# A graph layer and a mixture of experts in one program: three expert blocks move in among the node groups

## The chip, the cores and the metric

The program runs on one core of a Trainium2 chip. The metric is the device time of one execution, in microseconds (us); the kernel before takes 1253.61 us (median of three runs).

Engines: PE (TensorE, matmuls; its weight loads are shown as PEld), DVE (VectorE), ACT (ScalarE), POOL (GpSimd; it issues the indirect transfers) and SP (SyncE; it issues most of the plain transfers). Each engine takes its instructions strictly in the order in which the program lists them.

## The reference

What is computed, cut to what matters (6250 nodes, 100000 edges sorted by their target node `dst`):

```python
h = layernorm(x)                                  # 6250 x 256
s, cnt = segment_sum(edge, dst), segment_count(dst)   # edge: 100000 x 96
mx = where(cnt > 0, segment_max(edge, dst), 0)
z = concat([h, s, mx, s / max(cnt, 1), u[0]], 1)  # 256 + 3*96 + 64 = 608
x = x + (relu(z @ W1 + b1) @ W2 + b2 + h)         # hidden size 1024
q = layernorm(x)
v, idx = top_k(q @ gate_w + gate_b, 2)            # 16 experts
w = softmax(v)
f = [relu(q @ w1[e] + eb1[e]) @ w2[e] + eb2[e] for e in range(16)]  # 256 -> 512 -> 256
y = q + w[0] * f[idx[0]] + w[1] * f[idx[1]]
out = x + (layernorm(y) * gamma + beta)
```

## The kernel before, in words

**Node groups.** The 6250 nodes are 50 columns of P = 125. They are worked on in 13 groups of four columns (group 0 has two), and each group has 12 slots of a written schedule: slots 0 to 7 are `hidden` (L779 for 512 of the 544 inputs that differ from node to node, L796 for the last 32, the ReLU on ACT at L801; the 64 global inputs are folded into the bias once, `global_part`), slots 8 to 11 are `output` (L807), one column each. Around these stand the things that a group needs before it and does after it: the load of x (`take_x`, slot B - 17, with B the group's first slot), its layernorm (L717 scales a column into `xn` on ACT), two gathers per column on POOL (`take_edges` L737 into the tile `at`, `take_carry` L744 into `cg`), their join on DVE (`join_edges`, L750) and masking on ACT (`mask_edges`, L757), the five transposes (`turn`, L770) with ACT's copies into `inT` (L771); afterwards the residual on DVE (`residual`, L812), the second layernorm (`root_b` L821, `turn_b` L837), the gate's logits (`logits`, L845), the choice of two experts (`choose`, L852 to L860, with an exponential on ACT at L860), the place of each node among its experts' rows (`rank`, `rank_2`, `place`), and `send`, which scatters each node's row to its two experts' row buffers `xg_d` (POOL, L906).

**Edges.** DVE runs a stream of edge chunks beside this: running sums and maxima along runs of equal targets (L318 to L322, tiles `raw` and `rw`, in three buffers, each result stored to `rows_d`). At the end of each of seven regions a chain joins the runs: ACT's copies into `ct` (L394), transposes on PE (L406, L408), copies and a scan on DVE (L419, L423), transposes back (L432), DVE's correction (L438, L440) and a store of `carry_d` (L442), which later gathers read. Also spread among the groups is the search for the nodes' edges: `find_block` (ACT, L488), `take_blocks` (DVE, L492, and a POOL gather, L501), `find_edge` (ACT, L508), and `bounds`, `bounds_2` (PE, L526) and `index_nodes` (DVE, L642, reads PE's `pg` into `end`).

**The order** is written out by hand. Every piece is entered with a slot and, for some, a cost in DVE time; the entries are sorted by slot and listed in that order for all engines, and before each next slot the edge stream gets DVE time up to a credit of 4.6 us per slot:

```python
            at_slot(B + HC + i, output, g, i)
...
        tasks.sort(key=lambda t: t[:2])
...
            fn(*args)
            credit -= cost
```

**Experts.** All rows of an expert are worked on in blocks of SB = 256. `find_star` picks one favoured expert (the star) early; its rows are renumbered to stand first, and once groups 0 to 10 are counted (`count_full`, `take_full`) its first NA = 14 blocks can be run before the other experts' sizes are known. From the last output on, `run_block` takes one block after another, software-pipelined: `load_rows` (L1041: a register load on SP, then 263 KB from `xg_d`), `load_weights` (1026 KB, once for the star, for each block of another expert), `norm_block` (ACT), `turn_block` (L1074, copied at L1077), `first_layer` (L1192), `second_layer` (L1214), `own_place` (DVE, L1086 and L1087 for the star's weights `w`), `weigh` (DVE, L1115), `store_y` (SP, L1120), and then, for blocks of the others, the partner row of each row from `y_d`, the last layernorm and the scatter to `out`. A loop after the pipeline (`extra_block`) takes what blocks are left beyond the NS = 57 planned ones.

**Buffers.** PSUM has one bank for transposes (`pTp`) and five for accumulation (`acc`); `ld` holds `at` (two buffers), `xall` holds XB = 5 buffers of x, `wk` holds `xn` (one buffer) and `inT`.

## Time and profile before

| | |
|---|---|
| three runs | 1251.32, 1253.61, 1262.72 us; median 1253.61 |
| profiled execution | 1255.86 us; span on the core 1254.0 us |
| mean granted TensorE clock | 0.958 |
| busy: PE, PEld | 1103.0 us (88%), 784.4 us (63%) |
| busy: DVE, ACT, POOL | 976.0 us (78%), 603.8 us (48%), 565.8 us (45%) |
| HBM | 146.70 MB read, 121.75 MB written, 214 GB/s over the span |
| star's and others' first layer, L1192 | 912 matmuls, 206.8 us |
| second layer, L1214 | 912 matmuls, 208.8 us |
| groups' hidden layer, L779 | 832 matmuls, 367.2 us |
| groups' output, L807 | 800 matmuls, 190.2 us |
| first `hidden` of groups 3, 5, 6 | 247.6, 368.4, 428.4 us |
| last output ends | 800.9 us |

How to read it. Times of rows are from the start of the profiled span; the profiled execution took 1.9 us more than its span. The page's second part cuts the span into 40 slices of 31.35 us and gives the busy share of each engine as a digit in tenths. A row of the timeline is the start, the busy time, the engine, the line, the operation with out<-in, the shapes and the number of records; what stands in brackets is idle time ahead of it and what ended it. In the view of waits each row is a waiter and what it waits for, then the total in us, the count and the longest. A row of the chain is a start, a length and the work. "Releasers" are worked out from semaphore events. PE's matmuls are pipelined, so a busy PE is not always at its peak.

### The profile page before, as it was taken

To read this page: it belongs to the slowest core of one execution; us is meant where nothing else is said; L and a number is where in the kernel's file an instruction comes from. 1 tells how busy PE (TensorE), PEld (TensorE's weight loads), DVE (VectorE), ACT (ScalarE), POOL (GpSimd) and SP (SyncE) were. 2 spreads that over 40 slices of the span, in tenths; PEclk is the share of its full clock that TensorE was granted. 3 is DMA by queue.
4 is the path that set the end of the run, shared out by engine and by line. 5 is a ranking of instruction groups with operands and counts; after the bars stand their busy time and mean duration, and the time that the engine had idled before them with its cause. 6 is when DMAs were issued, how large, how long until landed. Compare 5 with 4: busy or idle time off the path is not lost.

```text
span 1254.0 us, 16849 instructions
## 1 busy us (share of the span) xinstructions
PE 1103.0 (88%) x4637; PEld 784.4 (63%) x4637; DVE 976.0 (78%) x2820; ACT 603.8 (48%) x1410; POOL 565.8 (45%) x721
## 2 busy tenths in 40 slices
PE   1594796997978888899999999999999999999983
PEld 1372363646454645466464665788888888888873
DVE  4689786996989888899989931355458888888985
ACT  3473252644255642434234252343367677766752
POOL 5121151673338673353733351303026666656664
PEclk9997899998989998999999999999999999999997
DMA  6959785787698898788999723113478889888972
GB/s 163 213 131 249 193 245 157 197 213 233 171 267 247 260 249 238 216 233 247 254 259 278 189 65 91 49 63 106 140 232 233 250 281 295 278 246 276 300 235 76
DMA packets 179318, 260.86 MB, mean 208 GB/s; under 512 B 35899, under 2 KB 145947, under 8 KB 173585
## 3 DMA queue, kind: packets, MB, share of 16 engines
q1 hardware_dynamic: 140097, 201.97, 56.3%
q0 software_dynamic: 39008, 57.35, 16.5%
q8 instruction: 37, 0.61, 0.2%
q14 instruction: 64, 0.52, 0.1%
q10 hardware_dynamic: 112, 0.41, 0.1%
HBM read 146.70 MB, written 121.75 MB: 214 GB/s over the span
## 4 chain that ended last, share of the span: by engine, by line
PE 40%; DVE 5%; DMA 5%; issue 1%; ACT 1%; POOL 0%; SPq 0%; another core or an unknown queue 0%; POOLq 0%; DVEq 0%
PE acc L1192 13%; PE acc L1214 13%; PE acc L779 6%; PE acc L807 4%; PE pT L1074 2%; DMA cg<-carry_d,next_i 2%; DMA xt<-in_x_dram 1%; DMA y_d<-yb 1%; PE pg L845 1%; PE acc L796 1%; DMA rows_d<-rw 0%; PE pT L770 0%; DMA g<-y_d,from_i 0%; DVE bsc L1142 0%; DVE yb L1115 0%
## 5 line engine op out<-in xcount | busy, mean ns | idle before, releaser
L779 PE MATMUL acc<-inT,w1x 128*128 128x500 f32 (+1 forms) x832 | 367.2, 589 | 4.8 <-DVE xt L812 4.8
L779 PEld LDWEIGHTS acc<-inT,w1x 128*128 128x128 f32 x832 | 158.7, 199 | 164.8 <-issue 150.9
L906 POOL DMA_INDIRECT xg_d<-xt,pos_i x100 | 135.1, 1351 | 249.1 <-issue 92.4
L1214 PE MATMUL acc<-wt,hb 128*128 128x256 f32 x912 | 208.8, 382 | 4.3 <-ACT hb L1200 4.1
L1192 PE MATMUL acc<-xT,wt 128*128 128x256 f32 x912 | 206.8, 380 | 1.6 <-DVE xT L1077 1.6
L807 PE MATMUL acc<-w2s,hT 128*125 128x256 f32 x800 | 190.2, 393 | 0.0
L1192 PEld LDWEIGHTS acc<-xT,wt 128*128 128x128 f32 x912 | 172.7, 190 | 25.1 <-DVE xT L1077 1.8
L1214 PEld LDWEIGHTS acc<-wt,hb 128*128 128x128 f32 x912 | 169.8, 191 | 26.8 <-ACT hb L1200 5.0
L807 PEld LDWEIGHTS acc<-w2s,hT 128*125 128x125 f32 x800 | 153.2, 196 | 24.8 <-issue 1.9
L1129 POOL DMA_INDIRECT g<-y_d,from_i x86 | 91.5, 1064 | 155.1 <-DMA y_d<-yb 134.3
L1200 ACT ACTIVATE hb<-acc,wt 128x256 f32<-128x256 f32 x200 | 84.0, 471 | 122.8 <-PE acc L1192 90.4
L501 POOL DMA_INDIRECT gb<-in_dst_dram,blk_i x50 | 75.7, 1514 | 98.8 <-ACT xt L725 41.7
L1165 POOL DMA_INDIRECT out_dram<-g,to_i x86 | 93.5, 1087 | 22.5 <-issue 18.3
L801 ACT ACTIVATE hT<-acc,c 128x500 f32<-128x500 f32 (+1 forms) x104 | 60.3, 662 | 71.5 <-PE acc L796 71.4
L1115 DVE SCALAR_TENSOR_TENSOR yb<-acc,w_b,xe 128x256 f32<-128x256 f32 x112 | 48.9, 478 | 47.5 <-PE acc L1214 38.3
L321 DVE TENSOR_TENSOR rw<-rw,raw 125x768 f32<-125x768 f32 x88 | 83.8, 952 | 0.2 <-issue 0.2
L322 DVE TENSOR_TENSOR rw<-rw,raw 125x768 f32<-125x768 f32 x88 | 83.6, 950 | 0.0
L318 DVE TENSOR_TENSOR rw<-rw,keep 125x768 f32<-125x768 f32 x81 | 76.8, 948 | 8.1 <-DMA rows_d<-rw 8.1
L744 POOL DMA_INDIRECT cg<-carry_d,next_i x44 | 64.0, 1455 | 33.8 <-issue 11.6
L737 POOL DMA_INDIRECT at<-rows_d,first_i x44 | 61.7, 1401 | 34.0 <-issue 20.5
L319 DVE TENSOR_TENSOR rw<-rw,bar 125x768 f32<-125x768 f32 x81 | 77.0, 950 | 0.0
L771 ACT COPY inT<-pT 128x500 f32<-128x500 f32 (+1 forms) x65 | 36.2, 556 | 83.0 <-PE pT L770 74.1
(324 smaller groups left out, 1591.4 us busy)
## 6 DMA issues: line engine op xcount, KB each, us to landing
wt<-in_wpack_dram SPq DMA_DIRECT2D x44, 1026.0 KB
rows_d<-rw SPq DMA_DIRECT2D x46, 960.0 KB
rows_d<-rw SPq DMA_DIRECT2D x46, 540.0 KB
raw<-in_edge_dram SPq DMA_DIRECT2D x46, 480.0 KB
xb<-xg_d SPq DMA_DIRECT2D x57, 263.0 KB
y_d<-yb SPq DMA_DIRECT2D x56, 256.0 KB
raw<-in_edge_dram SPq DMA_DIRECT2D x46, 270.0 KB
xt<-in_x_dram SPq DMA_DIRECT2D x12, 500.0 KB
```

What stands on the lines that cost most here:

```text
L318: nc.vector.tensor_tensor(su, prev[0], keep[c][:, :, s + j, None].to_broadcast(bcast), op=OP.mult)
L319: nc.vector.tensor_tensor(mx, prev[1], bar[c][:, :, s + j, None].to_broadcast(bcast), op=OP.min)
L321: nc.vector.tensor_tensor(su, su, x_j, op=OP.add)
L322: nc.vector.tensor_tensor(mx, mx, x_j, op=OP.max)
L779: nc.tensor.matmul(G[g]["pH"][m % 4][:, :n * P], w1x[:, k, m * 128:(m + 1) * 128], inT[:, k, :n * P], start=(k == 0), stop=False)
L807: nc.tensor.matmul(pO, G[g]["hT"][m][:, i * P:(i + 1) * P], w2s[:, m, :], start=(m == 0), stop=(m == HC - 1))
L906: d = nc.gpsimd.indirect_dma_start(out=xg_d[:, :], out_offset=IndirectOffsetOnAxis(ap=G[g]["pos"][:, i, k:k + 1], axis=0), in_=G[g]["xt"][ ...
L1129: d = nc.gpsimd.indirect_dma_start(out=g[:, h, :].bitcast(I32), out_offset=None, in_=y_d[:, :], in_offset=IndirectOffsetOnAxis(ap=BL[b]["f ...
L1165: d = nc.gpsimd.indirect_dma_start(out=out[:, :], out_offset=IndirectOffsetOnAxis(ap=BL[b]["to"][:, h:h + 1], axis=0), in_=BL[b]["g"][:, h ...
L1192: nc.tensor.matmul(pB[:, i, :], wt[:, k * FF + m * 128:k * FF + (m + 1) * 128], xT[:, k, :], start=(k == 0), stop=(k == DC - 1))
L1200: nc.scalar.activation(hb[:, m, :], pB[:, i, :], AF.Relu, bias=bias)
L1214: nc.tensor.matmul(to, hb[:, m, h * 128:(h + 1) * 128], wt[:, W2O + m * D:W2O + (m + 1) * D], start=(m == 0), stop=(m == FC - 1))
```

## The change

Three blocks of the star run among the node groups, one each in groups 3, 5 and 6 (`EARLY`), as entries of the schedule. In slot 3 of such a group `pick_early` counts the star's rows so far on PE and DVE and moves on by a block if there are enough; in slot 4 `load_early` loads that block's rows on SP; `norm_early` (ACT, and DVE for the weights), `turn_early`, `first_early` (two halves) and `second_early` (two halves of the rows) stand between slots 8.5 and 11.5, between the group's outputs; `store_early` issues the store of the block from ACT's queue. In `second_early` PE adds the row (a matmul with the identity) and the bias (a matmul of one contracted row) into the accumulator, where `weigh` does this on DVE for later blocks. These blocks use the transpose bank, the accumulation banks, and tiles of their own or of `gT`, `xn`.

The star now has NA = 17 blocks planned, 3 early and 14 after the groups; NS stays 57, so 40 others follow where 43 did. Its weights are loaded in slot 28 (`load_star`) into a tile that stays. `take_full` is done in two parts (the first 10 of the 14 blocks from the count of groups 0 to 10, the others from that of groups 0 to 11, after the last group's outputs are listed). To make room, x has four buffers where it had five, `at` one where it had two; the fill of the row buffers uses the early blocks' row tile. The weights of the global part (`w1u`) are loaded by SP into a buffer of `inT` later on, and the global part's matmuls and addition stand after the window sums.

```diff
-NA = 14
+KE = 3
+NA = KE + 14
+N1 = 10
+EARLY = (3, 5, 6)
 NS = 57
...
-XB = 5
+XB = 4
...
-    ld = mlp.enter_context(tc.tile_pool(name="ld", bufs=2))
+    ld = mlp.enter_context(tc.tile_pool(name="ld", bufs=1))
...
     def max_window(g, i):
         w = G[g]["win"][i]
+        if "at" not in G[g]:
+            G[g]["at"] = ld.tile([P, GS, 128 * (KC - DC + 1)], F32, name="at")
...
+    def load_star():
+        nc.vector.memset(done, float(SB))
+        e = nc.sync.value_load(star_i[0:1, 0:1], min_val=0, max_val=NE - 1)
+        nc.sync.dma_start(eba, eb2[ds(e, 1), :].to_broadcast([128, D]))
+        nc.sync.dma_start(wta, wpack[ds(e * 128, 128), :])
+
+    def pick_early(g):
+        pc = eps.tile([NR, NE], F32, name="ps")
+        nc.tensor.matmul(pc, ones[:P, :NR], M[:, NT - GRP[g - 2][0], :], start=True, stop=True)
+        nc.vector.tensor_scalar(more_f, pc[:, 0:1], done, float(SB), op0=OP.is_ge, op1=OP.mult)
+        nc.vector.tensor_add(done, done, more_f)
+        nc.vector.tensor_scalar(at_a, done[0:1], float(-2 * SB), 0.0, op0=OP.add, op1=OP.max)
+
+    def load_early():
+        EB["r"] = r = nc.sync.value_load(at_a[0:1, 0:1], min_val=0, max_val=(NA - 1) * SB)
+        nc.sync.dma_start(xba, xg_d[ds(r, SB), :].rearrange("(p h) d -> p h d", h=2))
+
+    def norm_early():
+        for h in range(2):
+            nc.scalar.activation(xba[:, h, 0:D], xba[:, h, 0:D], AF.Identity, scale=xba[:, h, D + 5:D + 6], bias=xba[:, h, D + 6:D + 7])
+        nc.vector.scalar_tensor_tensor(wea, xba[:, :, D + 2], float(N), xba[:, :, D + 1], op0=OP.is_ge, op1=OP.add)
+        nc.vector.tensor_tensor(wea, wea, xba[:, :, D], op=OP.min)
+
+    def turn_early():
+        pX = pTp.tile([128, DC, 2, 128], F32, name="pT")
+        for k in range(DC):
+            for h in range(2):
+                nc.tensor.transpose(pX[:, k, h, :], xba[:, h, k * 128:(k + 1) * 128], ident)
+        xT = gtp.tile([128, DC, GS * P], F32, name="gT", bufs=1).rearrange("p k n -> p (k n)")[:, 0:DC * SB]
+        EB["xT"] = xT.rearrange("p (k r) -> p k r", r=SB)
+        nc.scalar.copy(xT, pX.rearrange("p k h r -> p (k h r)"))
+
+    def first_early(half):
+        if half == 0:
+            EB["hb"] = wk.tile([128, GS, D], F32, name="xn", bufs=1)
+        pB = acc().rearrange("p (i r) -> p i r", i=2)
+        for i in range(2):
+            m = 2 * half + i
+            for k in range(DC):
+                nc.tensor.matmul(pB[:, i, :], wta[:, k * FF + m * 128:k * FF + (m + 1) * 128], EB["xT"][:, k, :],
+                                 start=(k == 0), stop=(k == DC - 1))
+            nc.scalar.activation(EB["hb"][:, m, :], pB[:, i, :], AF.Relu, bias=wta[:, B1O + m:B1O + m + 1])
+
+    def second_early(h):
+        if h == 0:
+            EB["pY"] = acc().rearrange("p (h d) -> p h d", h=2)
+        to = EB["pY"][:, h, :]
+        nc.tensor.matmul(to, ident, xba[:, h, 0:D], start=True, stop=False)
+        nc.tensor.matmul(to, ones[0:1, :], eba[0:1, :], start=False, stop=False)
+        for m in range(FC):
+            nc.tensor.matmul(to, EB["hb"][:, m, h * 128:(h + 1) * 128], wta[:, W2O + m * D:W2O + (m + 1) * D],
+                             start=False, stop=(m == FC - 1))
+        nc.scalar.activation(xba[:, h, 0:D], to, AF.Copy, scale=wea[:, h:h + 1])
+
+    def store_early():
+        EB["ra"] = nc.scalar.value_load(at_a[0:1, 0:1], min_val=0, max_val=(NA - 1) * SB)
+        d = nc.scalar.dma_start(y_d[ds(EB["ra"], SB), :].rearrange("(p h) d -> p h d", h=2), xba[:, :, 0:D].bitcast(I32))
...
-    def take_full():
-
-        full, nbi = MB["full"], MB["nbi"]
-        nc.vector.memset(full, 0.0)
-        nc.vector.tensor_copy(nbi, MB["pc"])
...
+    def take_full(a, z):
+
+        nbi, tf, last, top = MB["nbi"][:, 0:1], MB["tab_f"][:, a:z], MB["last"], MB["q"]
+        nc.vector.tensor_copy(nbi, MB["pc"][:, 0:1])
         nc.vector.tensor_scalar(nbi, nbi, 8, None, op0=OP.arith_shift_right)
...
+        nc.vector.tensor_scalar(top, nbi, 1.0, -1.0, op0=OP.mult, op1=OP.add)
...
+        nc.vector.tensor_scalar(tf, row_i[0:1, 0:z - a], last[0:1], top[0:1], op0=OP.add, op1=OP.min)
+        nc.vector.tensor_scalar(MB["tab_a"][:, a:z], tf, 0.0, float(SB), op0=OP.max, op1=OP.mult)
...
-                at_slot(max(0, B - 17), take_x, g)
+                at_slot(max(9, B - 17), take_x, g)
...
+        if g in EARLY:
+            for q, fn, *a in ((3, pick_early, g), (4, load_early), (8.5, norm_early), (9, turn_early), (9.5, first_early, 0),
+                              (10, first_early, 1), (11, second_early, 0), (11.5, second_early, 1), (12, store_early)):
+                at_slot(B + q, fn, *a)
...
+    at_slot(T, count_full, NG - 2)
+    at_slot(T + 1, take_full, N1, NA - KE)
+    at_slot(T, first_blocks, KE, NS)
+    for b in range(KE, NA):
+        at_slot(T + 1.6 * (b - KE), run_block, b, NS)
...
+        fill = xba[:, 0, :]
...
+    at_slot(SLOTS * EARLY[0] - 8, load_star)
...
-        nc.gpsimd.dma_start(w1u, w1[D + 3 * EF:D + 3 * EF + GF])
...
-        global_part()
+        w1u = wk.tile([128, KC + 1, GS * P], F32, name="inT").rearrange("p k n -> p (k n)")[:GF, 0:HID]
+        nc.sync.dma_start(w1u, w1[D + 3 * EF:D + 3 * EF + GF])
...
+        ps_u = global_part(w1u)
...
+        nc.vector.tensor_add(c1, ps_u, b1c)
```

## The prediction

> **What bounds the kernel now.** I read the page first: busy shares, then the 40 slices.
>
> ```profile
> PE 1103.0 (88%) x4637; PEld 784.4 (63%) x4637; DVE 976.0 (78%) x2820; ACT 603.8 (48%) x1410; POOL 565.8 (45%) x721
> DVE  4689786996989888899989931355458888888985
> PEclk9997899998989998999999999999999999999997
> ```
>
> The program has two stages: slices 6 to 22 are the node groups (DVE 8 to 9 tenths), after 800 us come the expert blocks. The page's average hides that they have different limits, so I cut the span into windows: group 5, group 9, and 227 us of late expert blocks (columns: length, busy time of PE, PEld, DVE, ACT, POOL, clock, DMA share, GB/s).
>
> ```profile
> 368.40:428.40 60.00, 51.05 (x194) 30.35 (x193) 50.87 (x128) 33.69 (x87) 41.77 (x39) 0.97 0.91 253
> 596.60:646.10 49.50, 48.46 (x194) 29.42 (x193) 48.44 (x106) 19.73 (x41) 23.66 (x26) 1.00 0.93 262
> 913.00:1140.00 227.00, 226.00 (x1108) 198.72 (x1108) 189.35 (x621) 156.23 (x361) 133.44 (x233) 1.00 0.85 263
> ```
>
> In the expert stage PE stands still for 1.0 of 227 us. The chain that ended last gives one block there:
>
> ```profile
> 1113.46 3.45 PE acc L1192 x16
> 1116.91 0.44 PE pT L1074 x4
> 1117.35 3.46 PE acc L1214 x16
> 1120.80 3.45 PE acc L1192 x16
> ```
>
> 3.45 + 0.44 + 3.46 = 7.35 us, and nothing but PE in it. In groups 3 to 7 neither engine is full, so I read who waits for whom between 368 and 486 us:
>
> ```profile
> DVE at L750 <- DMA cg<-carry_d,next_i: 11.0, 7, 3.6
> ACT dv L860 <- DVE I L857: 10.9, 1, 10.9
> PE pT L770 <- ACT inT L771: 8.9, 3, 4.0
> ```
>
> PE waits for ACT's copies, ACT waits (in its order) for DVE, DVE only for gathers: DVE leads and PE runs behind it by permission. PE idles 5.4 + 9.0 + 5.4 us in groups 3, 5 and 6. An extra PE task is free there as long as no DVE instruction that reads a PE result gets there first. That slack decides this case.
>
> **What goes.** Three expert blocks leave the PE-bound stage: 54 run after the groups instead of 57, still 14 of the favoured expert first, so 40 others instead of 43: 3 x 7.35 = -22.05 us. The loop after the pipeline stays empty by the reference's own routing: the favoured expert has 4831 rows (18 whole blocks, 17 taken), the rest need 40. Three 1026 KB weight loads go too; they lie under PE.
>
> **What comes, on PE.** Per early block: four transposes, 8 records of first layer per half, and per half of the rows 12 records (row, bias, second layer), at 0.216 us a record (3.46/16). The bias row has one contracted row; the nearest row is L796 (32 rows, cheaper), so 0.13 to 0.216, I take the latter. In the changed program's order, PE does after the second output (slot 9): transposes of the early block, turn k=2, first half, third output, first half, turn k=3, fourth output, row half, turn k=4, row half. So from the end of turn k=2 to the next group it needs 1.73 + 3.46 + 1.73 + 0.44 + 3.46 + 2.59 + 0.44 + 2.59 = 16.44 us. The early transposes wait for ACT's two scalings, which stand in ACT's order behind whatever ACT waits for. Group 5 before, PE then ACT:
>
> ```profile
> 415.92 3.62 PE L807 MATMUL acc<-w2s,hT 128*125 128x256 f32 x16
> 422.39 0.82 PE L770 MATMUL pT<-ident,at 125*128 125x125 f32 x4 [2.86 <-ACT inT L771]
> 423.00 5.17 PE L807 MATMUL acc<-w2s,hT 128*125 128x256 f32 x16
> 428.44 3.52 PE L779 MATMUL acc<-inT,w1x 128*128 128x500 f32 x8
> 431.91 0.37 PE L408 MATMUL ps<-ident,ct 125*96 125x125 f32 x2
> 440.23 0.46 PE L432 MATMUL ps<-ident,st 96*125 96x96 f32 x2 [0.38 <-DVE st L423]
> 421.59 0.27 ACT L394 COPY ct<-rw 125x96 f32<-125x96 f32 x1 [0.59 <-DVE rw L322]
> 424.59 0.63 ACT L488 ACTIVATE junk<-b1r,nhalf 125x400 bf16<-125x400 f32 x1
> ```
>
> ACT is free for the scalings at 421.86, when its copy for the edge chain (L394) is done. Scalings 2 x 0.52 (L717: 2.08 for four), transposes 0.82 (the cold row at 422.39), copy 0.65, turn 0.82: 425.2. Plus 16.44, plus 0.9 for records that run slow after the gap (423.00: 5.17 against 3.62; four of them fall here) gives 442.5 where group 6 began at 428.4: PE is late by 14.1 us. The third output, which used to fill the wait for ACT, now comes after it.
>
> Who waits next is DVE, by its rows there:
>
> ```profile
> 428.74 0.14 DVE L492 TENSOR_SCALAR blk_f<-acc 125x4 f32<-125x4 f32 x1
> 438.65 0.27 DVE L419 COPY kk<-ps 96x125 f32<-96x125 f32 x1
> 444.20 0.95 DVE L438 TENSOR_TENSOR tmp<-ps,kp 125x768 f32<-125x768 f32 x1
> ```
>
> L492 needs ACT's third L488, now behind the early ReLUs: first half done 433.0, two ReLUs 0.94, copy 0.6, L508 and L488 1.5: 436.1, DVE late 7.4. L419 needs L408, at 432.3 + 14.1 = 446.4; DVE comes at 446.1: 7.8. L438 needs L432, at 454.4; DVE comes at 452.0: 10.2. From there choosing (460.7, logits done 450.3) has room.
>
> Groups 3 and 6, in the same way: ACT is free at 297.2 and 478.2, PE late by 13.8 us each. But the residuals read outputs 11.5 to 16 us after they end, and the first sharp point is L642 (end<-pg), behind one hidden chunk (3.46) and two small matmuls (1.0): 322.3 against DVE's 319.8, and 503.4 against 501.4: 2.5 and 2.0 in all. PE had waited 2.5 and 2.9 us for DVE there, and gets the rest back at the turns (6.8 us idle at 350, 3.8 at 528).
>
> A rule of the Trainium skill speaks against the change here. "TensorE: Matmul & The Clock Gate", Part 1 (The HAM clock gate), says that PE falls to half clock after an idle window of some 3.4 us. This trace is harsher: the 2.86 us gap above already made 16 records 1.55 us longer, while 2.01 us at 406.8 did not. By the rule alone the group 5 of before would have lost nothing, and my estimate of its delay would be 1.5 us larger.
>
> **Small parts.** DVE gains five tiny operations per block at 0.16 us (L1086, L1087): 0.8 in group 5 (those of 3 and 6 are in the 2.5 and 2.0). SP's register load and 263 KB block load (L1041: 0.27 to 0.98, then the issue) stand before edge loads with three buffers; it issues near 279, 399 and 456, while the sends it needs end at 263.4, 388.0 and 446.2, and ACT wants the rows 18 us later. ACT's register load and store (some 1.6 us) come before the table load for the next root, where ACT waited 10.3 and 10.9 us. The favoured expert's 1026 KB move to about 217 us, into 9 us in which SP issues nothing: 4.5 us of transfer at 226 GB/s, under the edge buffers: 0, and 4.5 without that cover. One buffer for at: the next gather starts at least 10.8 us after the last turn that reads it (646.3, 657.1): 0; late PE in group 5 is met by a gather that is late too. Four x buffers: the load of group 7 (407.6) follows the sends of group 3 (388.0) by 19.6 us: 0. The global part: 3.57 us of PE move from 29.5 to 54.3, into 3.9 us of idle: 0; -1 (L526 comes 0.9 earlier) to +3.6 (its weights late behind the window gathers). Second count: nine small operations in slices where DVE is 1 to 3 tenths busy: 0 to 1.5.
>
> **Sum.** -22.05 + 2.5 + 10.2 + 0.8 + 2.0 = -6.6. DVE's later waits may give a little back (1.7 us at 532.8 for a gather of an old region): 0 to 1.7, I take 0.9. -7.5 on the profiled execution: 1255.86 - 7.5 = 1248.4. That execution is 2.25 above the median 1253.61, so 1246.1 there.
>
> **Rivals.** (1) The delay is swallowed. After 455 us DVE waits 3.60 + 1.10 + 1.55 + 1.69 + 0.83 + 3.21 = 12.0 us for gathers and an x load. If those are set by DMA and not by DVE's own work, the 10.2 of group 5 vanish: -22.05 + 5.3 = -16.7, median 1236.9. For: DMA share 0.91. Against: the gather of 469 us follows a store (L442) that follows DVE's L440, behind the late L438. (2) Slower: PE's lateness is paid in full in all three groups, because the single transpose bank and ACT's order chain PE to ACT to DVE at more points than I priced: 13.8 + 14.1 + 13.8 - 22.05 = +19.6, median 1273. It decides from 7.35 us a block on. For: group 5 shows such points, one with 3.5 us of slack (L438). Against: in groups 3 and 6 the least is 8.6. (3) The picks find too few rows, do a block twice, and the saved blocks run after all: -22.05 falls away, +14.6, median 1268. Against: 572, 1371 and 1763 rows are there when 512, 768 and 1024 are wanted.
>
> **Chances.** Forecast 0.50 (own range 1240 to 1253: stalls of 9 to 21 us), rival 1 0.34, rival 2 0.12, rival 3 0.04. One per cent, 12.5 us, is about what a measurement tells here. Faster by more: most of rival 1 and the low edge of the forecast, 0.36; slower: rival 3 and most of rival 2, 0.12; within: 0.52. The range takes in all of rival 1 (down to -22, 1232) and the partly paid cases of rival 2 (to 1262).
>
> **What would show it.** Right: 54 blocks of L1192's kind, still 7.35 apart; PE waiting for ACT's scalings before the early transposes, longest in group 5 (some 8 us); DVE held behind L492, L419 and L438's counterparts by some 10 us; L642's by 1 to 2; the last group ending near 815 instead of 801. Wrong: no DVE wait after group 5's block (rival 1's side), or waits for outputs and logits in groups 3, 4, 6 and 7 (rival 2's).

## The result, and the profile after

The changed kernel takes 1266.68 us (median of 15 runs, 1255.11 to 1272.98) against 1254.05 us for the kernel before on the same chip (15 runs, 1251.32 to 1264.53): a ratio of 1.0085, with a 95% interval of 1.0065 to 1.0106, or 10.7 us more. The forecast was 1246.1 us and its range ended at 1262. The profiled execution, the longest of the 15, took 1272.98 us, its span is 1271.2 us, and its mean granted clock 0.951.

The page of the kernel after, busy shares, then the rows of DVE and of the granted clock from the 40 slices (each 31.8 us now). Line numbers are each kernel's own: L807 of the kernel before is L819 here, L770 is L782, L771 is L783, L642 is L654, and L492, L419 and L438 are L501, L428 and L447.

```profile
PE 1115.7 (88%) x4669; PEld 789.4 (62%) x4669; DVE 959.4 (75%) x2784; ACT 599.1 (47%) x1401; POOL 561.7 (44%) x696
...
DVE  5599686987789667799998973145546889887875
...
PEclk9896898997999799999999999999999999999996
```

PE works 12.7 us more than before and DVE 16.6 us less. The thin stretch ahead of the experts' blocks, where DVE falls to 1 to 5 tenths, begins one slice later, and many of the digits ahead of it are lower than they were.

The windows of the kernel after for group 5, group 9 and 225 us of late expert blocks (length, busy time of PE, PEld, DVE, ACT, POOL, clock, DMA share, GB/s):

```profile
375.20:457.40 82.20, 67.69 (x240) 41.72 (x239) 63.33 (x167) 39.42 (x100) 62.56 (x56) 0.88 0.85 228
627.80:677.30 49.50, 48.55 (x195) 29.52 (x194) 48.44 (x106) 19.68 (x41) 22.89 (x25) 1.00 0.95 261
945.00:1170.00 225.00, 224.69 (x1101) 197.56 (x1100) 186.44 (x610) 155.09 (x358) 130.58 (x229) 1.00 0.86 267
```

Group 9 and the expert stage are what they were. Group 5 takes 82.2 us where it took 60.0, and its clock fell from 0.97 to 0.88. The chain that ended last, kernel after, one block:

```profile
1124.53 3.45 PE acc L1271 x16
1127.98 0.44 PE pT L1153 x4
1128.42 3.46 PE acc L1293 x16
```

Again 7.35 us. So the expert stage kept its price per block, and the time was lost among the groups. With each group counted from its first hidden matmul to the next group's (one profiled execution each):

| group | 3 | 4 | 5 | 6 | 7 | sum |
|---|---|---|---|---|---|---|
| before, us | 56.5 | 64.3 | 60.0 | 56.7 | 60.5 | 298.0 |
| after, us | 77.6 | 50.5 | 82.2 | 72.1 | 48.7 | 331.1 |
| PE idle before | 5.4 | 9.9 | 9.0 | 5.4 | 6.6 | 36.3 |
| PE idle after | 12.2 | 1.4 | 14.5 | 7.9 | 0.0 | 36.0 |
| granted clock before | 0.97 | 0.89 | 0.97 | 0.97 | 0.92 | |
| granted clock after | 0.91 | 1.00 | 0.88 | 0.93 | 1.00 | |

All other groups together differ by 1.0 us, and the last output ends at 833.0 instead of 800.9 us. The three groups with a block got 58.7 us longer, the two without became 25.6 us shorter. That second number has a floor: in group 7 PE now never stands still. It is made of two parts: in groups 4 and 7 PE's idle time fell from 16.5 to 1.4 us, and its busy time from 108.3 to 97.8 us, mostly because 20.0 us of it had been at half clock and none is now.

Over all five groups PE idles as long as before, 36.0 us against 36.3, and works 33.4 us longer, 27.2 of which are the blocks' records at full rate. So the blocks' work did not fill PE's idle time; it came on top of it.

The waits of DVE, kernel after, groups 3 to 7 (what waits, for what, total, count, longest):

```profile
DVE at L762 <- DMA cg<-carry_d,next_i: 25.5, 9, 8.7
DVE end L654 <- PE pg L536: 11.9, 2, 5.9
DVE xt L824 <- PE acc L819: 7.9, 4, 3.9
DVE kk L428 <- PE ps L417: 5.7, 1, 5.7
DVE tmp L447 <- PE ps L441: 2.1, 1, 2.1
DVE bsa L709 <- DMA xt<-in_x_dram: 2.0, 1, 2.0
```

Before, the same stretch had 23.6 us for the gathers `cg`, 2.9 for an x load, 0.2 for a store, and nothing for PE. Now 27.6 us are for PE: `bounds_2` (L654), the outputs (L824), the edge chain (L428, L447). And the longest waits of PE there:

```profile
PE pT L976 <- ACT xba L968: 13.5, 4, 7.1
PE pT L782 <- ACT inT L783: 12.8, 4, 8.4
PE acc L988 <- ACT xn L990: 3.4, 6, 0.6
```

Group 5 shows how this comes about. PE, kernel after (start, busy time, line, out<-in, shapes, records; in brackets the idle time ahead and what ended it):

```profile
421.12 3.67 PE L819 MATMUL acc<-w2s,hT 128*125 128x256 f32 x16
431.91 1.39 PE L976 MATMUL pT<-ident,xba 128*128 128x128 f32 x4 [7.11 <-ACT xba L968]
433.97 1.10 PE L782 MATMUL pT<-ident,at 125*128 125x125 f32 x4 [0.68 <-ACT gT L979]
434.86 1.92 PE L988 MATMUL acc<-gT,wta 128*128 128x256 f32 x4
437.35 2.08 PE L988 MATMUL acc<-gT,wta 128*128 128x256 f32 x4 [0.56 <-ACT xn L990]
439.22 5.15 PE L819 MATMUL acc<-w2s,hT 128*125 128x256 f32 x16
444.20 1.03 PE L988 MATMUL acc<-gT,wta 128*128 128x256 f32 x4
445.79 1.13 PE L988 MATMUL acc<-gT,wta 128*128 128x256 f32 x4 [0.56 <-ACT xn L990]
...
447.19 3.62 PE L819 MATMUL acc<-w2s,hT 128*125 128x256 f32 x16
...
457.44 1.00 PE L791 MATMUL acc<-inT,w1x 128*128 128x500 f32 x2
```

And ACT in front of it:

```profile
426.94 0.63 ACT L497 ACTIVATE junk<-b1r,nhalf 125x400 bf16<-125x400 f32 x1
...
430.21 0.27 ACT L403 COPY ct<-rw 125x96 f32<-125x96 f32 x1 [2.55 <-DVE rw L330]
431.08 0.27 ACT L403 COPY ct<-rw 125x96 f32<-125x96 f32 x1 [0.60 <-DVE rw L331]
431.26 1.09 ACT L968 ACTIVATE xba<-xba 128x256 f32<-128x256 f32 x2
433.33 0.59 ACT L979 COPY gT<-pT 128x512 f32<-128x512 f32 x1 [0.99 <-PE pT L976]
```

The scalings (L968) stand in ACT's order behind two copies into `ct` (L403), which wait for DVE's edge sums until 430.21 and 431.08. PE has done its output at 424.8, so its early transposes start after a gap of 7.11 us. The records that follow are slow: 16 of L819 take 5.15 us at 439.22 and 3.62 us at 447.19. Four windows of 4 us, kernel after, show the clock (the 0.50 ahead of the DMA share):

```profile
432.00:436.00 4.00, 3.31 (x11) 2.44 (x12) 3.73 (x21) 1.82 (x5) 2.66 (x4) 0.50 0.96 273
436.00:440.00 4.00, 3.44 (x8) 2.24 (x8) 3.79 (x18) 1.74 (x6) 3.54 (x5) 0.50 0.94 239
440.00:444.00 4.00, 4.00 (x15) 3.24 (x14) 0.47 (x3) 0.00 (x0) 3.17 (x5) 0.71 0.96 224
444.00:448.00 4.00, 3.44 (x18) 2.72 (x17) 2.95 (x11) 1.51 (x4) 0.82 (x1) 1.00 0.96 296
```

The clock stays at half for some 10 us from PE's restart on, although PE is busy 3.3 to 4.0 of every 4.0 us. Short waits break this stretch: 0.68 us for ACT's copy (L979) and 0.56 us for the ReLU (L990), since the second pair of a half's matmuls goes into the bank that the ReLU reads. "TensorE: Matmul & The Clock Gate", Part 1 (The HAM clock gate), of the Trainium skill has the full clock come back after some 3.4 us of sustained busy time. Here it came back at about 442.3 (0.71 on average between 440 and 444: half until 442.3, full from there), 5.0 us after the last of these waits and 10.4 us after PE had started again. Sized by the page's figure from the restart on, the slow stretch would have been a third as long (an estimate). The kernel before has the same with fewer waits, first in group 4, then in group 5:

```profile
310.00:314.00 4.00, 3.28 (x9) 2.19 (x10) 3.79 (x16) 0.00 (x0) 3.34 (x6) 0.51 0.79 164
314.00:318.00 4.00, 4.00 (x8) 1.71 (x7) 3.93 (x7) 0.30 (x1) 3.56 (x5) 0.64 0.44 108
422.00:426.00 4.00, 3.61 (x12) 2.96 (x13) 3.73 (x20) 3.25 (x10) 1.30 (x2) 0.59 1.08 266
426.00:430.00 4.00, 4.00 (x18) 2.90 (x17) 3.79 (x18) 1.33 (x4) 3.34 (x5) 0.98 1.05 357
```

In group 4 PE started again at 310.16 after a gap of 2.54 us and waited once more, 0.56 us until 311.73; by the 0.64 the full clock came at about 316.9, 5.2 us after that wait and 6.8 after the restart. In group 5 it started again at 422.39 after 2.86 us and waited no more; by the 0.59 and 0.98 the full clock came at about 426.1, 3.7 us after the restart. That the short waits hold the clock down is read from these three stretches; no run changed the waits and nothing else.

### The profile page after: what moved, and what is told of

Same layout as the page of the kernel before. It is cut to its first block, busy times and chain, and to the rows that moved or that the text cites. A ratio compares the mean times of both kernels' runs of the same rounds, so it can differ in the third digit from the quotient of the medians.

```text
span 1271.2 us, 16795 instructions
## 1 busy us (share of the span) xinstructions
PE 1115.7 (88%) x4669; PEld 789.4 (62%) x4669; DVE 959.4 (75%) x2784; ACT 599.1 (47%) x1401; POOL 561.7 (44%) x696
## 3 DMA queue, kind: packets, MB, share of 16 engines
q0 software_dynamic: 38352, 57.09, 16.5%
## 4 chain that ended last, share of the span: by engine, by line
PE 37%; DVE 6%; DMA 4%; issue 2%; POOL 1%; ACT 1%; SPq 0%; another core or an unknown queue 0%; POOLq 0%; DVEq 0%; ACTq 0%
PE acc L1271 13%; PE acc L1293 12%; PE acc L791 6%; PE acc L819 3%; PE pT L1153 2%; DMA rows_d<-rw 1%; DMA xt<-in_x_dram 1%; POOL xg_d L918 1%; DMA out_dram<-g,to_i 1%; DMA cg<-carry_d,next_i 1%; PE pg L857 1%; DVE bsc L1221 0%; DMA g<-y_d,from_i 0%; DVE g L1216 0%; PE pT L782 0%
## 5 line engine op out<-in xcount | busy, mean ns | idle before, releaser
L918 POOL DMA_INDIRECT xg_d<-xt,pos_i x100 | 131.8, 1318 | 246.4 <-issue 92.1
L819 PE MATMUL acc<-w2s,hT 128*125 128x256 f32 x800 | 189.0, 392 | 0.0
L819 PEld LDWEIGHTS acc<-w2s,hT 128*125 128x125 f32 x800 | 152.8, 195 | 24.8 <-issue 1.9
L1208 POOL DMA_INDIRECT g<-y_d,from_i x80 | 86.3, 1079 | 155.0 <-DMA y_d<-yb 136.4
L1271 PE MATMUL acc<-xT,wt 128*128 128x256 f32 x640 | 146.9, 382 | 6.6 <-ACT xT L1156 6.6
L1293 PE MATMUL acc<-wt,hb 128*128 128x256 f32 x640 | 146.6, 381 | 3.1 <-ACT hb L1279 3.1
L1271 PEld LDWEIGHTS acc<-xT,wt 128*128 128x128 f32 x640 | 122.6, 192 | 23.9 <-ACT xT L1156 7.0
L510 POOL DMA_INDIRECT gb<-in_dst_dram,blk_i x50 | 89.8, 1796 | 106.4 <-ACT xt L737 43.2
L1293 PEld LDWEIGHTS acc<-wt,hb 128*128 128x128 f32 x640 | 118.9, 191 | 19.5 <-ACT hb L1279 4.7
L1279 ACT ACTIVATE hb<-acc,wt 128x256 f32<-128x256 f32 x160 | 66.8, 468 | 74.5 <-PE acc L1271 39.6
L1244 POOL DMA_INDIRECT out_dram<-g,to_i x80 | 85.0, 1063 | 21.4 <-issue 17.3
L813 ACT ACTIVATE hT<-acc,c 128x500 f32<-128x500 f32 (+1 forms) x104 | 60.1, 660 | 72.1 <-PE acc L808 72.1
L327 DVE TENSOR_TENSOR rw<-rw,keep 125x768 f32<-125x768 f32 x81 | 76.8, 948 | 11.8 <-DMA rows_d<-rw 11.8
L1194 DVE SCALAR_TENSOR_TENSOR yb<-acc,w_b,xe 128x256 f32<-128x256 f32 x106 | 46.3, 478 | 48.9 <-PE acc L1293 32.7
L756 POOL DMA_INDIRECT cg<-carry_d,next_i x44 | 63.1, 1435 | 26.6 <-issue 11.6
L783 ACT COPY inT<-pT 128x500 f32<-128x500 f32 (+1 forms) x65 | 36.2, 557 | 70.3 <-PE pT L782 63.3
```

Source lines behind the costliest of these rows:

```text
L327: nc.vector.tensor_tensor(su, prev[0], keep[c][:, :, s + j, None].to_broadcast(bcast), op=OP.mult)
L510: nc.gpsimd.indirect_dma_start(out=gbs_[t], out_offset=None, in_=dst_b, in_offset=IndirectOffsetOnAxis(ap=blk_i[:, t:t + 1], axis=0))
L819: nc.tensor.matmul(pO, G[g]["hT"][m][:, i * P:(i + 1) * P], w2s[:, m, :], start=(m == 0), stop=(m == HC - 1))
L918: d = nc.gpsimd.indirect_dma_start(out=xg_d[:, :], out_offset=IndirectOffsetOnAxis(ap=G[g]["pos"][:, i, k:k + 1], axis=0), in_=G[g]["xt"][ ...
L1208: d = nc.gpsimd.indirect_dma_start(out=g[:, h, :].bitcast(I32), out_offset=None, in_=y_d[:, :], in_offset=IndirectOffsetOnAxis(ap=BL[b]["f ...
L1244: d = nc.gpsimd.indirect_dma_start(out=out[:, :], out_offset=IndirectOffsetOnAxis(ap=BL[b]["to"][:, h:h + 1], axis=0), in_=BL[b]["g"][:, h ...
```

## The experiments

Theory A, in its first form: PE gets late by its hand-overs through ACT's order, DVE pays at the few points that read PE soonest, and listing these pieces sooner brings the time back. Three rivals: the other parts of the edit cost the time (one buffer for `at`, four for x, the moved loads); the amount of PE work in these groups does; or, rival D, the blocks disturb each other.

**All of the change but the blocks.**

```diff
-KE = 3
+KE = 0
-EARLY = (3, 5, 6)
+EARLY = ()
```

> The changed kernel with no early block at all (KE = 0, EARLY empty, 57 blocks after the groups; the star's weights still loaded in slot 28, four x buffers, one at buffer, the global part where the change puts it, the count in two parts). Theory A: these do nothing: 1254 plus or minus 3. Rival C (buffers, the weight load or the second count cost something): 1258 to 1275, with longer waits of DVE for gathers or x rows, or a longer stage of experts.

1.0003 (0.9973 to 1.0033); groups 3 to 7 take 292.7 us. The first rival falls: the buffers, the moved loads, the second count and the moved global part are together worth nothing that the time shows, give or take 4 us. In the trace group 1 took 89.0 us where it had 79.4, and 4.1 us of that are left at the last output (805.0). Another profile of the kernel before tells whether this is the run or the change:

> The kernel before once more, for a second profile: group 1 took 79.4 us in its first one and 82 to 92 in those of the changed kernel and its variants, which share the early x load, the fill and the weights of the global part. If the changed kernel does that, it takes 79 to 81 again; if it is the run, 85 to 92.

1253.31 us; group 1 took 80.9, groups 3 to 7 295.4 us. So it goes with the change: group 1 takes 79.4 to 81.4 us in the three profiles of the kernel before and its one variant, and 81.6 to 92.2 us in the seventeen of the changed kernel and its variants. The run times show no loss from it.

**One block at a time** (group 3, 5 or 6, with 56 blocks after the groups).

```diff
-KE = 3
+KE = 1
-EARLY = (3, 5, 6)
+EARLY = (3,)    # (5,), (6,)
```

> The changed kernel with one early block, in group 3 (KE = 1, EARLY = (3,), 56 blocks after the groups). Theory A (each DVE wait for a PE result behind the early block is paid in full, and nothing else is): -7.35 for the block, +5.9 for the wait at L654, +0.5 for an output: -1, ratio 0.999. Rival B (PE's whole lateness of some 20 us is paid): +13, ratio 1.010. Rival D (the loss comes from two early blocks in neighbouring groups 5 and 6): -7, ratio 0.994.

> The changed kernel with one early block, in group 5. Theory A: -7.35, +7.2 for the outputs, +7.8 for the edge chain (L428, L447): +7.7, ratio 1.006. Rival B: +15, ratio 1.012. Rival D: -2 to 0, ratio 0.999.

> The changed kernel with one early block, in group 6. Theory A: -7.35, +5.9 for L654, +0.2 for an output: -1, ratio 0.999. Rival B: +8, ratio 1.006. Rival D: -7, ratio 0.994. The three single ratios less one should add up to that of the changed kernel (+0.0085) by theory A, to much less by rival D.

1.0088 (1.0056 to 1.0120), 1.0106 (1.0073 to 1.0139) and 1.0020 (0.9994 to 1.0045). With the 7.35 us that each saves, a block costs 18.4, 20.6 and 9.9 us, 48.9 in all, where the three together cost 10.7 + 22.05 = 32.7. Rival D falls: alone the blocks are no cheaper. Theory A's ratios (0.999, 1.006, 0.999) were too low in all three; rival B's 1.010 and 1.012 are near the first two. By the times the blocks are even cheaper together than alone, but groups 3 to 7 do not say so: alone they get 10.4, 17.6 and 7.2 us longer, 35.2 in all, and together 33.1; the rest of the difference lies outside these groups (group 1 takes 88.8 to 92.2 us in these three profiles). The lengths show where lateness comes back: after the block of group 3 (75.9 us, 19.4 more) group 4 takes 51.5 instead of 64.3 us; after that of group 5 (82.4 us, 22.4 more) group 6 gives back only 5.2 (51.5 instead of 56.7) and group 7, at 60.8, nothing.

**Sooner bounds.** `bounds_2` is listed 1.5 slots sooner, in the kernel after and in the kernel before.

```diff
-        at_slot(T, bounds_2, b)
+        at_slot(T - 1.5 if b > GW + 1 else T, bounds_2, b)
```

> Only the two small matmuls behind L654 (end<-pg) move, for the blocks whose nodes start at groups 4 and 7: in PE's order from behind the next group's first hidden chunk to ahead of the fourth output and the two row halves of the early block. Theory A: DVE's two waits of 5.9 us at L654 vanish and DVE keeps most of it, since it leads in these groups: 9 to 12 us less, 1255 to 1258. Rival B (PE full): DVE comes earlier but finds the next output or logits late, 0 to 4 less, 1263 to 1267.

> The kernel before, with only the two small matmuls behind L642 (end<-pg; L526, L527) moved ahead of the fourth output, as in e2. In the profile of before DVE does not wait at L642 at all. Theory A (the wait exists only because of the early block): no change, ratio 1.000. Rival: the groups 8 to 12, which took 247 us in e2, e3 and e5 and 255 in before, get the same gain without any early block: 7 us less, ratio 0.994.

After: 1.0013 (0.9978 to 1.0047), 9 us less, as theory A had it; the L654 waits are gone. Before: 1.0023 (1.0002 to 1.0044), no gain, as theory A also had it, because DVE did not wait there. But groups 3 to 7 went only from 331.1 to 327.3: waits on outputs (8.2 us) and the edge chain (7.8) stayed. The other part, groups 8 to 12 at 247.3 us instead of 254.7, has no explanation here; the kernel before with the same edit has 255.0. Group 4 and group 7 are 48.5 and 48.3 us now with PE idle 0.0: here PE itself is the bound. In the kernel before the edit makes lateness that costs these groups nothing: PE stands 9.8 and 10.2 us for DVE at the small matmuls, groups 3 and 6 take 64.7 and 70.6 us (8.2 and 13.9 more), and groups 4 and 7 give it back (52.5 and 48.3), so that the five take 297.1 us where they took 298.0.

**Scalings and transposes sooner**, so that ACT reaches them ahead of the copies into `ct`; alone, with the sooner bounds, and with the second layer moved into the next group as well.

```diff
-            for q, fn, *a in (..., (8.5, norm_early), (9, turn_early), ...
+            for q, fn, *a in (..., (6.9, norm_early, 0), (7.4, turn_early), (8.5, norm_early, 1), ...
...
-                              ... (11, second_early, 0), (11.5, second_early, 1), (12, store_early)):
+                              ... (13, second_early, 0), (14, second_early, 1), (14, store_early)):
```

> ACT's two scalings of the early block move from slot 8.5 to 6.9 and its transposes with their copy from slot 9 to 7.4, so that both stand before the last joins' masks and the copies into ct; nothing else moves. Theory A (the loss is PE's late start: PE stands 7.1 us in group 5 and 5.1 us in group 6 waiting for ACT's scalings, then runs its next records slowly, some 4 to 7 us more, and DVE pays for that lateness at four places): the wait before the early transposes falls below 1 us, DVE's waits for outputs and the edge chain in group 5 (15.0 us) fall to about 3, the one of 5.9 us after group 6 to about 0, the one after group 3 by 2: some 18 to 20 us less, 1247. Rival B (PE is simply full: 9.1 us of early work do not fit into groups with 5.4 to 9.0 us of idle time, at whatever place): the waits move from one row to the next, the time falls by less than 6, above 1261. Rival C (fewer buffers for x and at are the cause): no change, 1264 to 1269.

> Both moves together: scalings and transposes of the early block earlier, and the two small matmuls ahead of the fourth output. Theory A: 1247 less what is left of the L654 waits (about 4): 1243, and the last output ends near 808 us where it ended at 833 in the changed kernel. Rival B: above 1255. Rival C: 1264 to 1269.

> As e3_both, and the two row halves of the early block's second layer, with its store, move from slots 11 and 11.5 into the next group's hidden layer (slots 13 and 14), so that PE comes 5.2 us earlier to the next hidden layer and to the edge chain's transposes (L415, L417, L441). Theory A: the waits at L428 and L447 (5.7 and 2.1 us) vanish and nothing takes their place: 7 to 9 us less than e3_both, ratio 0.993. Rival B (PE's total work decides, wherever it is put): no change against e3_both, ratio 1.000.

1.0032 (1.0011 to 1.0054), 0.9999 (0.9973 to 1.0024) and 1.0005 (0.9978 to 1.0033); groups 3 to 7 take 322.2, 320.4 and 325.5 us. The first gained 6.6 us where 18 to 20 were expected, and both together give 1253.9 us on the scale of the first comparison (0.9999 x 1254.05), 11 more than the 1243 expected. The waits of PE with both edits, groups 3 to 7:

```profile
PE pT L976 <- ACT inT L783: 16.5, 3, 7.5
PE pT L782 <- ACT inT L783: 10.6, 3, 7.3
```

The gap moved. Now ACT reaches the scalings before the block's rows have landed (they were asked for after the picks, and SP's transfer took 9.18 us in group 5), stands there, and the next turn's copy (L783), which must empty the one transpose bank, comes late. With the second layer later, the wait of L428 vanished; that of L447 grew, and one for ACT (L839) came in:

```profile
DVE xt L824 <- PE acc L819: 6.7, 4, 3.0
DVE tmp L447 <- PE ps L441: 4.2, 1, 4.2
...
DVE xt L839 <- ACT xt L833: 3.4, 2, 2.9
```

So the simple form of theory A falls: each move takes a wait away and brings up others, and the best of them gained 10.8 us (0.9999 against 1.0085) of the 32.7 that the blocks cost.

A place between the two was tried, and then the same with only two blocks:

```diff
-            for q, fn, *a in (..., (6.9, norm_early, 0), (7.4, turn_early), ...
+            for q, fn, *a in (..., (7, norm_early, 0), (8, turn_early), ...
...
-EARLY = (3, 5, 6)    # second kernel only
+EARLY = (3, 6)
```

> The changed kernel in a third order: ACT's scalings of the early block directly behind the hidden layer's last ReLUs (slot 7), its transposes on PE behind the first output, with ACT's copy of them ahead of the last two masks and of the copies into ct (slot 8), and the two small matmuls of L654 ahead of the fourth output. In e1 and e3 ACT stood at the scalings until the block's rows were there, and PE's transposes waited for the bank; here an output lies between each two steps. Theory H: PE's idle time in groups 3 to 7 falls from 36 to about 20 us and its clock stays up: 8 to 12 us less than before, ratio 0.990 to 0.994. Theory W: as e3, 1.000.

> e7 with two early blocks, in groups 3 and 6 alone (KE = 2, 55 blocks after the groups), since group 5 has the points with the least slack (outputs, L428, L447). Theory H: -14.7 and 5 to 8 of stalls: 7 to 10 less than before, ratio 0.992 to 0.994. Theory W: 1.000 or more.

1.0016 (0.9985 to 1.0047) and 0.9990 (0.9956 to 1.0025): both miss. No order of these that computes the whole result is clearly faster than the kernel before.

**PE's work alone.** No early blocks; instead PE gets matmuls on constants into a spare bank in groups 3, 5 and 6, which nothing reads and which wait for nothing.

```diff
+    def more_pe(n):
+        to = acc()[:, 0:D]
+        for i in range(n):
+            nc.tensor.matmul(to, ident, w2s[:, i % HC, :], start=(i == 0), stop=(i == n - 1))
...
+        if g in (3, 5, 6):
+            for q, k in ((9, 8), (10, 8), (11, 24)):    # ((2, 10), (3, 10), (4, 10), (5, 10)); ((9, 4), (10, 4), (11, 12))
+                at_slot(B + q, more_pe, k)
```

> The kernel of e4 (no early block, 57 blocks after the groups) with 40 more matmuls of 128 rows by 256 (8.6 us at 0.216 us a record) in each of groups 3, 5 and 6, into a bank that nobody reads, with constants as operands: 8, 8 and 24 records in slots 9, 10 and 11, between and behind the outputs, where the change puts its early work. Nothing waits for ACT, DVE or a load. Theory A (PE has slack there; the loss is the hand-overs to ACT, the slow clock after them and the single DVE waits): PE is 8.6 us late, of which only L428 and the outputs of group 5 feel 2 to 5: ratio to before 1.003. Theory B (PE's idle time in these groups is the wait of a loop through DVE and is not free): most of 25.9 us is paid, 20 to 26: ratio 1.017 to 1.021.

> The same 40 records a group, but 10 each in slots 2 to 5, among the hidden layer's chunks. Theory A: 2 to 6 us, since PE waits at the turns later in the same group anyway: ratio 1.003. Theory B: the same as d1_dummy_out, 1.017 to 1.021; if it is much lower than d1, the place decides and not the amount.

> As d1_dummy_out with half its work: 20 matmuls (40 records, 8.6 us, the early block's own amount) in each of groups 3, 5 and 6, at slots 9, 10 and 11 (4, 4 and 12), no early block, 57 blocks after the groups. Theory H: the first part of the work finds PE's idle time: 3 to 8 us of 25.9, ratio 1.002 to 1.006. Theory W: as the early blocks cost (about 22 even with the better order of e3): ratio 1.015 to 1.02.

The first two were given twice the dose that their text counts, because a matmul of this size is two records (the matmuls counted in the table ahead of the prediction are such records too): 240 records, 51.8 us at 0.216. They cost 1.0162 (1.0128 to 1.0197) and 1.0111 (1.0084 to 1.0137): 20.3 us among the outputs, 13.9 among the hidden layers. With the right dose, 120 records or 25.9 us, it is 1.0055 (1.0024 to 1.0085), 6.9 us (3 to 11), and groups 3 to 7 take 298.6 us, as before: PE's idle time there falls from 36.3 to 21.5 us. So PE does take the work of three blocks for a quarter of its length; the amount of work explains a fifth of the 32.7 us (a tenth to a third by the interval).

**The hand-overs taken apart.** First the matmuls of the early blocks read constants, without the transposes and ACT's copy of them; then the ReLUs and the output copies go too.

```diff
-                nc.tensor.transpose(pX[:, k, h, :], xba[:, h, k * 128:(k + 1) * 128], ident)
...
-        nc.scalar.copy(xT, pX.rearrange("p k h r -> p (k h r)"))
...
-                nc.tensor.matmul(pB[:, i, :], wta[...], EB["xT"][:, k, :],
+                nc.tensor.matmul(pB[:, i, :], wta[...], w2s[:, k, :],
...
-        nc.tensor.matmul(to, ident, xba[:, h, 0:D], start=True, stop=False)
+        nc.tensor.matmul(to, ident, w2s[:, h, :], start=True, stop=False)
...
-            nc.tensor.matmul(to, EB["hb"][:, m, h * 128:(h + 1) * 128], wta[...],
+            nc.tensor.matmul(to, w2s[:, m, h * 128:(h + 1) * 128], wta[...],
...
-            nc.scalar.activation(EB["hb"][:, m, :], pB[:, i, :], AF.Relu, ...)    # second kernel only
-        nc.scalar.activation(xba[:, h, 0:D], to, AF.Copy, scale=wea[:, h:h + 1])    # second kernel only
```

> The changed kernel with the early blocks' matmuls fed from constants: the four transposes and their copy are left out, the first layer reads the second weight matrix where it read the transposed rows, the second layer reads it where it read rows and hidden values, so the three early blocks' results are no longer those of the reference. Loads, scalings, ReLUs, output copies, stores and DVE's small operations stay, but PE waits for none of them. Theory H (the hand-overs PE to ACT to PE, and the slow clock after them, are the loss): the three blocks save 22 and cost what 25.9 us of pure PE work cost, 4 to 10: ratio 0.986 to 0.990. Theory W (PE's work or the work on ACT, SP and DVE is the loss): ratio 1.000 or more.

> h1_no_handover without ACT's reads of the early blocks' accumulators too: no ReLU and no output copy (left out as well as what h1 leaves out), so PE waits for no bank; loads, scalings, DVE's small operations, stores and all matmuls but the transposes stay, and 54 blocks follow the groups. Theory H (the hand-over through ACT's queue, now the bank's, is the loss): the three blocks save 22, cost 7 for PE's work (h2) and 4 to 6 for the gather issue that stands in group 3: ratio 0.990 to 0.994, groups 5 to 7 at 180 to 186 us where h1 took 197. Theory W (ACT's, SP's and DVE's other work): as h1, 1.002 to 1.005.

1.0036 (1.0003 to 1.0069), a miss against 0.986 to 0.990; then 0.9891 (0.9800 to 0.9982), near what was expected (groups 5 to 7 take 185.6 us, expected 180 to 186). Without rows to wait for, PE still waits in group 5, as ACT and PE of the first kernel show:

```profile
434.90 0.27 ACT L403 COPY ct<-rw 125x96 f32<-125x96 f32 x1 [3.05 <-DVE rw L330]
...
435.95 1.09 ACT L968 ACTIVATE xba<-xba 128x256 f32<-128x256 f32 x2
436.94 0.55 ACT L783 COPY inT<-pT 128x500 f32<-128x500 f32 x1
...
439.29 0.45 ACT L986 ACTIVATE xn<-acc,wta 128x256 f32<-128x256 f32 x1
```

```profile
430.16 1.03 PE L984 MATMUL acc<-w2s,wta 128*128 128x256 f32 x4
439.80 2.08 PE L984 MATMUL acc<-w2s,wta 128*128 128x256 f32 x4 [8.61 <-ACT xn L986]
```

The first two matmuls are done at 431.2. The ReLU (L986) stands in ACT's order behind the same copies into `ct`, the scalings, a turn's copy and `find_edge`, which waits for a gather: it runs at 439.29, and the next two matmuls, into the same bank, have waited 8.61 us. One hand-over was cut and the next one in line held as long. Without the reads none of PE's waits is for the early block any more; the longest in groups 3 to 7 are those for the turns' copies:

```profile
PE pT L782 <- ACT inT L783: 13.9, 4, 7.9
```

Set beside each other, groups with a block and groups without, in us, from one profile each. "Slow" is PE's busy time in groups 3, 5 and 6 above that of before (153.4) and above the block's records at full rate (25.9; 27.2 with transposes), so it holds half clock, the drawn-out ends of pairs that stop alone (1.03 us for the four records at 444.20 above, where 4 x 0.216 is 0.86), and the pick's matmul:

| kernel | groups 3, 5, 6 | PE idle in them | slow | groups 4, 7 | PE idle in them | sum |
|---|---|---|---|---|---|---|
| before | 173.2 | 19.8 | | 124.8 | 16.5 | 298.0 |
| PE's work alone (half dose) | 188.0 | 12.0 | -3.3 | 110.6 | 9.4 | 298.6 |
| blocks, no reads by ACT | 205.5 | 21.5 | 4.7 | 101.8 | 3.8 | 307.3 |
| blocks, constants as input | 221.5 | 30.1 | 12.1 | 99.8 | 1.9 | 321.3 |
| after | 231.9 | 34.6 | 16.7 | 99.2 | 1.4 | 331.1 |

Read downwards: each hand-over adds idle time and, with it, slow records. Of the 16.7 us in the last row 11.8 are half clock: in these three groups PE worked 33.7 us at half clock where it had worked 10.1, and half of each is lost. Read across: groups 4 and 7 give back until PE is full there, 96.8 us in the fullest case (sooner bounds), 28.0 us under the kernel before; lateness beyond that cannot come back in them. By the times, three blocks cost 6.9 us for PE's work, 8.4 with their loads, scalings and the rest (0.9891 gives -13.7, and 22.05 are saved; its interval leaves -3 to 20), 26.6 with ACT reading PE's banks (4.5 + 22.05) and 32.7 as they are. The steps come from runs on different chips, and the last two ratios' intervals touch; the order agrees with that of the traces. One rival stays in the step from 8.4 to 26.6: without its reads ACT also has 18 operations of 0.47 us less to do, and no run keeps that work on ACT while PE need not wait for it. What speaks for the hand-over is PE's waits for the ReLUs, 12.3 us in groups 3 to 7 in the kernel that has them, 8.6 of them in the rows above.

**The pick of the rows** left out, the block of group 3 alone, its address fixed:

```diff
-        nc.vector.memset(done, float(SB))
+        nc.vector.memset(done, float(2 * SB))
+        nc.vector.memset(at_a, 0)
...
-            for q, fn, *a in ((3, pick_early, g), (4, load_early), ...
+            for q, fn, *a in ((3, int), (4, load_early), ...
```

> s3_group3_alone without the pick in group 3: no matmul and none of the three small DVE operations (L957 to L960); the row address is the constant 0, which is what the pick gives, set when the star's weights are loaded, so SP's register load waits for nothing either. Theory K (the three DVE operations shift DVE's unbroken run of adds against POOL's gather, whose issue then stands until that run ends): the issue takes 1.4 us again, ACT's wait for gb in group 3 falls from 9.3 to about 3 us, groups 3 and 4 take 120 to 123 us where they took 127.4, ratio 1.002 to 1.005 where s3 had 1.0088. Rival L (the block's 263 KB load delays the gathers): the long issue stays, 1.007 to 1.010.

1.0047 (1.0005 to 1.0089), which does not part from the 1.0088 (1.0056 to 1.0120) with the pick. Groups 3 and 4 take 125.3 us against 127.4, more than the 120 to 123 expected. What the pick does to POOL stands in the last section, and it reaches PE: in the kernel after, ACT's `find_edge` in group 3 stood 6.87 us for a gather that POOL issued late, the turn's copy behind it came late, and PE waited 8.4 us, its longest wait in groups 3 to 7. So that wait is no hand-over of the block. With the block of group 3 alone that wait of PE is 4.3 us, and without the pick 1.9; ACT's wait for such gathers falls from 9.3 to 2.5 us. Yet PE's waits for the edge chain and the scalings grow, from 1.9 to 3.1 and from 1.0 to 2.8 us, and group 3 takes 74.8 us against 75.9.

## Why the prediction was wrong

- **What goes, -22.05 us: right.** Over seven profiles with 57 blocks after the groups the expert stage averages 451.0 us, over eight with 54 blocks 430.9: -20.1. (Single profiles scatter: the two shown give 453.1 and 438.1, -15.0.)
- **How late PE gets in groups 3, 5 and 6: this step failed.** Predicted 13.8 + 14.1 + 13.8 = 41.7 us, measured 58.7 (21.1, 22.2, 15.4). Of the 41.7, 27.2 were the block's records, 2.7 slow records and the rest, 11.8, waiting. Measured: 27.2, 16.7 and 14.8. The term for slow records, 0.9 a group, was sized from four records after a 2.86 us gap, although I had foretold a gap of some 8 us myself; in group 5 the gap is 7.11 us, and the half clock lasts 10.4 us from the restart on, with short waits for ACT in it. The experiments with constants show that slow records come with the hand-overs, not with the matmuls: -3.3 us with matmuls alone, 12.1 with ACT reading their banks. Behind this stands the sentence that an extra PE task is free in PE's idle time. It held nearly for work that waits for nobody; with the blocks the idle time of the five groups stayed at 36 us.
- **What is given back: right in size, for a reason that I did not see.** I had 41.7 - 14.7 = 27.0 us, measured 25.6. I took it as DVE's slack at single points; it came back in groups 4 and 7, as 15.1 us of PE's idle time and 10.5 us of busy time at a higher clock, and there PE has 28.0 us to give and no more. With 27 of 28 already spent in the forecast, errors in the lateness had to show. That the two sizes agree is luck.
- **Which waits of DVE show it: half right.** L428 and L447 were named, with DVE 10.2 us late behind the last of them; they waited 5.7 + 2.1 = 7.8 us, and the outputs' readers, 3.9 and 3.3 us in group 5, come on top. L501 did not wait. (The 433.0 that the prediction calls the end of the first half is by its own list that of the second.) The two waits at L654, in groups 4 and 7, were named at 2.5 and 2.0 and took 5.9 each.
- **The wait for ACT's scalings** was foretold as some 8 us in group 5 and took 7.1; this wait was right, its price was not. I counted the hand-over once, as serial durations with ACT free. PE waits for ACT again at each half's ReLU and at each turn.
- **Small parts at nothing: right** in the time, 1.0003, though group 1 takes up to 13 us more in the profiles. The pick is not among them: about 5 us by the medians, 2 by the groups, and not distinguishable from nothing.
- **Rival 1** fell: DVE's waits for `cg` are 25.5 us against 23.6, so the gathers moved along with the lateness and swallowed none. **Rival 3** fell: 54 blocks ran. **Rival 2** had the cause, the single transpose bank and ACT's order chaining PE to ACT to DVE at more points than priced, and a number (1273) nearer than the forecast's; that rival 3's 1268 is nearer still is chance. Its form, everything paid and nothing given back, was not what happened: more was late than it said, and 25.6 us came back. Its sign, waits for outputs and logits in groups 3, 4, 6 and 7, hardly showed (0.5 and 0.2 us).

What stays open: how much of the 26.6 - 8.4 us between the two kernels with constants is the half clock and how much the waiting. In the table it is 7.4 us of slow records and 8.6 of idle time, less 2.0 that groups 4 and 7 give back more, but the two always come together here, and which brings which along was not tested; a bank for each half's pairs, so that no ReLU stands between its matmuls, was not tried.

## What to carry to other kernels

In this kernel PE's idle time took extra work only where that work waited for nobody: 25.9 us of matmuls on constants cost 6.9 us, and as many with ACT reading their results between them (loads and scalings included) cost 26.6, almost four times that. Before moving such work, list each hand-over with what the other engine's order holds in front of it, and price the slow restart together with the wait; then look up how much the stretches after it can give back before their own engine is full, since what goes beyond that is paid. Five other orders of the three blocks gained 7 to 11 us of the 32.7 and none is clearly faster than the kernel before; when each wait taken away brings up others, count all hand-overs of the place before trying a further order. Whether another place would do better was not tried.

## What the runs showed of the hardware

A gather's issue on POOL took seven times its usual time. POOL in group 3, kernel after, then in the kernel with one block and no pick:

```profile
265.88 1.29 POOL L749 DMA_INDIRECT at<-rows_d,first_i  x1 [0.30 <-issue]
267.47 9.74 POOL L510 DMA_INDIRECT gb<-in_dst_dram,blk_i  x1 [0.30 <-issue]
277.52 1.20 POOL L510 DMA_INDIRECT gb<-in_dst_dram,blk_i  x1 [0.30 <-issue]
```

```profile
271.15 1.28 POOL L749 DMA_INDIRECT at<-rows_d,first_i  x1 [0.30 <-issue]
272.74 1.43 POOL L510 DMA_INDIRECT gb<-in_dst_dram,blk_i  x1 [0.30 <-ACT xn L729]
```

In all ten profiles that have a pick in group 3 one issue there takes 9.7 us; in the nine others, and in the one where only the pick was left out, it takes 1.2 to 1.5. The long one starts 0.03 us after DVE's last pick operation (267.30 to 267.44) and lasts over ten of DVE's edge operations without a gap (267.37 to 276.13). "SBUF — State Buffer" (SBUF: two separate sides) in the Trainium skill has DVE and POOL share a pair of ports as an exclusive lock, held for a whole instruction; DVE takes it in a two-port mode or, against an operation of POOL that reads SBUF, with two SBUF inputs, as its edge operations here have. The same section says that POOL cannot write the descriptors of a transfer that it issues while DVE runs an operation in a two-port mode. A row of 9.74 us that ends 1.08 us after DVE's run would fit a lock that POOL does not get in between; the issues of 1.43 us beside the same kind of operations in the kernels without the pick do not fit. What decides between the two was not found.
